# Four layers on one core: layer 0's output products moved into layer 1, transposes of layers 2 and 3 sent through DRAM

## The chip, the core and the metric

The kernel runs on one core of a Trainium2 chip. The metric is device time in microseconds of one execution, the median of several. The engines are PE (matrix products), DVE (vector), ACT (activations), POOL (general vector work) and SP, which here issues almost every DMA. Each works through its own list of instructions in order and waits on semaphores that others raise.

## What is computed

Four transformer-like layers on 8 blocks of 512 tokens with 128 features, all in float32; each layer is attention and then a feed-forward part, each on a layer-normed copy of x and added back to x.

```python
x = x + _L0_attn_ref(_layernorm(x), ...)  # spiking attention with batch norm
x = x + _L0_ffn_ref(_layernorm(x), ...)   # 8 heads x 16 small experts, the best two weighted; out @ Wo + bo
x = x + _L1_attn_ref(_layernorm(x), ...)  # linear attention
x = x + _L1_ffn_ref(_layernorm(x), ...)   # gated part and one of 8 experts on 256 chosen tokens
x = x + _L2_attn_ref(_layernorm(x), ...)  # softmax attention, 16 heads of 64
x = x + _L2_ffn_ref(_layernorm(x), ...)   # top 2 of 8 low-rank experts on the first 1024 tokens
x = x + _L3_attn_ref(_layernorm(x), ...)  # a causal convolution of 21 taps
x = x + _L3_ffn_ref(_layernorm(x), ...)   # gated part whose inputs and weights are rounded to FP4
```

In `_L3_ffn_ref` every group of 16 numbers is scaled by its largest and rounded to one of 15 values, for x (128 wide), for the weights (352 x 128) and for the hidden h (352 wide).

## The kernel before

x stays in SBUF as eight tiles x[b] of 128 partitions x 4 x 128: token row p, tile j, feature. A product needs features on the partitions, so every normed block is transposed first: four 128x128 transposes on PE by the identity (into one bank) and an ACT copy of 128x512 out of the bank.

**Layer 0's feed-forward part** is a loop over 128 units (b, e), 16 experts for each of 8 blocks (lines 689 to 706). A unit's `first_half` multiplies h by w1 (four 32-row products, four banks) and lets ACT apply Gelu in two instructions (L569 on one bank, L570 on three); `second_half`, two units later, multiplies by w2, DVE scales by the gates (L582), and POOL adds to acc[b] (L588). `finish(b)` multiplies acc[b] by Wo and adds the result to x[b] (L274); it runs in unit (b+1, 4), in a bank lent from the three that the next unit's `first_half` needs, and for the last block after the loop. There the very last product of unit 127 is not added to acc by POOL, but multiplied by Wo on its own. The gates of `choice` (steps of DVE work, one a unit, five in each of the first two) come back from DRAM, spread over partitions, by 8 DMAs for every 4 units (L550).

**Layer 1** runs rounds i over a list of stages (lines 1217 to 1238): each stage works on block i + lag, so a block's attention takes several rounds. `stats` (lag 2) is the first to read x[b].

**Layers 2 and 3** (`late`) are 64 frames n = 8 b + c (block b, pair c of heads). Per frame, in the order in which PE sees it (lines 2601 to 2619): `scores(n, 0)`, hook "V", `context(n-1)`, hook "G", `scores(n, 1)`, hook "D", `project(n)`, hook "E". Hooks hold work of other parts, put there by hand with `at(frame, hook, function)`:

- `norm_steps`: statistics, scaling on ACT, transposes (`turn_`, L1472, ACT copy L1473). `new_xt(b)` makes layer 2's input of block b this way; `project(8b-2)` is the first to need it.
- `planned(b, start)`: layer 3 of block b; start is 13, 20, 27, 34, 41, 48, 56, so three blocks are always at different stages. In frames counted from start: norm at 0 and 1, convolution taps at 2 to 4, `conv_out` and new statistics at 5, rounding of x (`quant_x1`, `quant_x2`) at z-2 and z-1, its transposes (`turn_x`, L2089) at z-1, gate products at z to z+3, rounding of h in two halves at z+1 to z+4, h turned, `down` and the store at z+6. z is 10 for the "wide" blocks 0 to 4.
- `weights_in_frames`: the weights of layer 3 are rounded in frames 1, 2 and 4 and transposed a frame later (`turned_w`, L2435 and L2445).

For the wide blocks h already goes another way: `blocks_h` lets DVE transpose within 32x32 blocks (L2154) and SP write the blocks to their places in DRAM by four DMAs in pieces of 128 bytes (L2158); `fetch_h`, a frame later in the same hook, reads the turned h back.

`project(n)` and `gate_steps` use halves of PE's rows. Their second half on the same bank must not overtake the first, and SP is the messenger:

```python
def mark(ins):
    m = nc.sync.nop(nofuse=True).ins
    tc.add_manual_dep(m, ins.name, SYNC)
    return m
```

The nop waits on SP for the last product of a first half; PE's next half waits for the nop. `gate_steps` are called inside `scores(n, 0)` (hook "S"), after about half of it.

Of the kernel before, what the change touches and what calls it, by code (L numbers as in the profile page):

```python
# [25 lines left out]
P = 128  # L26
D = 128
# [137 lines left out]
def body(ctx, tc, dram, spans, x_in, ib, it, ic, ei, out):  # L165
# [113 lines left out]

    def layer0():  # L280
# [7 lines left out]
        with ExitStack() as st:  # L288
# [7 lines left out]
            acc = once.tile([P, NB, TB], F32, tag="acc", name="acc")  # L296
# [46 lines left out]
            def scale(b, own=3):  # L343
                l0[b]["xn"] = xn = norm.tile([P, J, D], F32, tag="xn", name="xn")
                nb, rs = l0[b]["by"]
                scaled(xn, x[b], (nb, rs), own)
                for j in range(own, J):
                    r1, n1 = rs[:, j : j + 1], nb[:, j : j + 1]
                    nc.gpsimd.tensor_scalar(xn[:, j, :], x[b][:, j, :], r1, n1, ALU.mult, ALU.add)
# [89 lines left out]
            def exponentials(b):  # L439
                nc.scalar.activation(acc[:, b, :], depth[:, b, :], AF.Exp)  # L440

            def choice(b):


                d, ex = by_expert(depth, b), by_expert(acc, b)
# [43 lines left out]
            with (  # L489
# [8 lines left out]
                def run(stages, iterations):  # L498
                    for i in iterations:
# [20 lines left out]
                        (lambda b: scale(b, J), -1),  # L520
# [52 lines left out]
            def second_half(b, e, hm, gs):  # L573
                po = bank()
                for i in range(4):
                    mm(
                        po[32 * i : 32 * (i + 1), :],
                        w2[:, e, :, :].rearrange("p a o -> p (a o)"),
                        hm[:, i, :],
                    )  # L580
                pr = acc[:, b, :] if e == 0 else wp.tile([P, TB], F32, tag="pr", name="pr")
                nc.vector.scalar_tensor_tensor(  # L582
                    pr, po, f0["b2"][:, e : e + 1], gs, ALU.add, ALU.mult
                )
                if (b, e) == (NB - 1, 15):
                    l0[b]["last"] = pr
                elif e > 0:
                    nc.gpsimd.tensor_tensor(acc[:, b, :], acc[:, b, :], pr, ALU.add)  # L588

            def finish(b):  # L590
                terms = [(lambda j: acc[:, b, j * P : (j + 1) * P], f0["wo"])]
                if "last" in l0[b]:
                    terms.append((lambda j: cols(l0[b]["last"], j), f0["wo"]))
                add_to_residual(b, by_token(terms, None))
# [48 lines left out]
            with tc.manual_schedule():  # L643
# [36 lines left out]
                def second(n):  # L680

                    if n >= 2:
                        b, e = units[n - 2]
                        second_half(b, e, hms.pop(n - 2), gs[(n - 2) // 4][:, e % 4, :])
                        fetch(n - 1)
                    for _ in range(1 if n > 1 else 5):
                        side("V", n)

                for n in range(len(units) + 2):
                    first(n)  # L690
                    if n >= len(units):

                        banks["own"] = threes[0][:, 1 + n - len(units), :]
                        second(n)
                        banks.pop("own")
                        continue

                    banks["own"] = threes[(n + 1) % 2][:, 0, :]
                    b, e = units[min(n, len(units) - 1)]
                    if e == 4 and b > 0:  # L700
                        finish(b - 1)
                    else:
                        side("P", n)
                    banks.pop("own")
                    second(n)
                finish(NB - 1)
# [124 lines left out]
    def layer1():  # L831
# [9 lines left out]
        with tc.tile_pool(name="l1", bufs=2) as wp, tc.tile_pool(name="l1c", bufs=1) as once:  # L841
# [372 lines left out]
            def chosen_put():  # L1214
# [13 lines left out]
                (project_kv, 0),  # L1228
                (z_turn, -7),
# [9 lines left out]
            with tc.manual_schedule():  # L1239
# [13 lines left out]
                nought = once.tile([P, J, D], F32, tag="nought", name="nought")  # L1253
# [152 lines left out]
    def late():  # L1406
# [11 lines left out]
        with tc.tile_pool(name="a2", bufs=2) as wp, tc.tile_pool(name="l3", bufs=1) as lp:  # L1418
# [3 lines left out]
            steps = {}  # L1422

# [6 lines left out]


            def norm_steps(b, dst, bias=None, part=(0, J)):
# [41 lines left out]

                return stats, scale, turn_, t
# [512 lines left out]
            def layer3(b, xp, tile_, part=(0, J), conv_bank="one", h_tag="h"):  # L1988
# [96 lines left out]

                def turn_x():
                    ps = bank()
                    for j in range(j1 - j0):
                        nc.tensor.transpose(cols(ps, j), cols(t["xq"], j), ident)  # L2089
                    t["xt"] = xt = tile_("xt", block("xt3", 2))[:, lo:hi]  # L2090
                    nc.scalar.copy(xt, ps[:, :n])
# [53 lines left out]
                def quant_h2_tile(i, j):  # L2145
                    sc, a = t["fh", i]
                    k = slice(22 * j, 22 * (j + 1))
                    h = tile_("h", h_tile)
                    fp4_round(lp, h[:, 2 * i + j, :], sc[:, k], a[:, k, :], 22)
# [76 lines left out]
                stats, scale, turn_, _ = norm_steps(  # L2226
                    b, lambda: xp()[:, pad + lo : pad + hi], "b3", part
                )
                stats2, scale2, _, t2 = norm_steps(b, None, None, part)
                return SimpleNamespace(t=t, **{k: v for k, v in locals().items() if callable(v)})  # L2230

            def planned(b, f0_):
# [7 lines left out]
                plan = [  # L2240
                    (1, "V", s.stats) if b == 1 else (0, "E", s.stats),
                    (1, "G", s.scale),
                    (1, "E", s.turn_),
# [12 lines left out]
                else:  # L2256
# [15 lines left out]
                    (6, "E", s.quant_x1) if early else (z - 2, "V", s.quant_x1),  # L2272
                    (z - 1, "V", s.quant_x2),
                    (z - 1, "E", s.turn_x),
                ]
                for j in range(J):
# [10 lines left out]
                    (h_ + 4, "V", lambda: s.quant_h2(1)),  # L2287
                ]
                if wide:
                    plan += [  # L2290
                        (z + 2, "E", lambda: s.blocks_h(0)),
                        (z + 3, "E", lambda: s.fetch_h(0)),
                        (z + 4, "E", lambda: s.blocks_h(1)),
                        (z + 5, "E", lambda: s.fetch_h(1)),
                        (z + 6, "E", s.down),
# [12 lines left out]
            for b in range(1, NB):  # L2308
                stats, scale, turn_, _ = norm_steps(b, new_xt(b), "lb")
                n = {1: 3, 2: 6, 3: 14, 4: 26, 5: 33, 6: 40, 7: 47}[b]  # L2310
                at(n, "V" if b < 4 else "E", stats)
                at(n + 1, "G", scale)
                at(n + 1, "E", turn_)
# [24 lines left out]
            def end():  # L2338
# [63 lines left out]
                B.quant_h2_tile(1, 0)  # L2402
                B.quant_h2_tile(1, 1)
# [5 lines left out]
            def weights_in_frames():  # L2409
# [20 lines left out]
                def turned_w(name):  # L2430
                    ps = bank()
                    w_ = wq[name]
                    if name == "down":
                        for i, at_ in thirds:
                            nc.tensor.transpose(  # L2435
                                ps[:C3, i * P : (i + 1) * P], w_[:, at_ : at_ + C3], ident
                            )
                        wt["down"] = const.tile([P, 3, P], F32, tag="wd", name="wd")
                        nc.vector.tensor_copy(
                            wt["down"][:C3], ps[:C3, : 3 * P].rearrange("p (i n) -> p i n", i=3)  # L2440
                        )
                        nc.vector.memset(wt["down"][: C3 - thirds[1][1], 1:, :], 0.0)
                    else:
                        for i, w in chunks:
                            nc.tensor.transpose(  # L2445
                                ps[:, i * P : i * P + w], cols(w_, i)[:w], ident[:w, :w]
                            )
                        wt[name] = const.tile([P, I3], F32, tag="wt_" + name, name="wt_" + name)
                        nc.vector.tensor_copy(wt[name], ps[:, :I3])
# [101 lines left out]
                for frame, name in ((1, "gate"), (2, "up"), (4, "down")):  # L2551
                    at(frame, "V", lambda name=name: rounded(name))
                    at(frame + 1, "E", lambda name=name: turned_w(name))
# [30 lines left out]
            with tc.manual_schedule():  # L2584
# [16 lines left out]
                for n in range(N):  # L2601
# [17 lines left out]
                    weigh(n, 1)  # L2619
                    hook(n, "E")  # L2620
# [57 lines left out]
```

## Time and profile before

| | us |
|---|---|
| three timed runs | 1400.63, 1401.19, 1397.15 |
| median | 1400.63 |
| the profiled execution | 1393.95 |
| its span, first to last instruction | 1392.2 |
| busy: PE, DVE, ACT, POOL | 1327.5, 1014.3, 1014.6, 642.4 |
| layer 0's unit loop | about 104 to 382 |
| layer 1 | about 386 to 500 |
| frames of layers 2 and 3 | about 504 to 1334 |

A matmul's record includes its latency (a 128-column transpose lasts 0.27 us, but four of them start 0.11 us apart), so the stages are judged by the distance of starts, not by busy time. In the timelines a line's first number is its start in us from the span's start, then its duration, engine, line, operation, output<-input, shapes and count; in brackets stands how long the engine had been idle before it and whose event ended that. In rows by line, the numbers after the bar are total busy us and mean ns, then the idle time before and its causes.

### The profile page before, as it was taken

To read this page: it belongs to the slowest core of one execution; us is meant where nothing else is said; L and a number is where in the kernel's file an instruction comes from. 1 tells how busy PE (TensorE), PEld (TensorE's weight loads), DVE (VectorE), ACT (ScalarE), POOL (GpSimd) and SP (SyncE) were. 2 spreads that over 40 slices of the span, in tenths; PEclk is the share of its full clock that TensorE was granted. 3 is DMA by queue.
4 is the path that set the end of the run, shared out by engine and by line. 5 is a ranking of instruction groups with operands and counts; after the bars stand their busy time and mean duration, and the time that the engine had idled before them with its cause. 6 is when DMAs were issued, how large, how long until landed. Compare 5 with 4: busy or idle time off the path is not lost.

```text
span 1392.2 us, 33106 instructions
## 1 busy us (share of the span) xinstructions
PE 1327.5 (95%) x12935; PEld 706.1 (51%) x12935; DVE 1014.3 (73%) x2148; ACT 1014.6 (73%) x2060; POOL 642.4 (46%) x748
## 2 busy tenths in 40 slices
PE   7889999999989999999999999999999999999997
PEld 3762222222267655547447545555555545555576
DVE  6785556666467778863783778888788797887876
ACT  7869999999978656665684686787767867667632
POOL 6645666666632533330472353353443634424432
PEclk9999999999999999999999999999999999999999
DMA  5019999999681010031211101101011010010000
GB/s 180 1 27 139 141 126 127 132 127 133 85 272 32 28 40 24 16 108 33 60 31 38 45 2 22 30 2 33 20 22 24 9 33 20 19 27 9 2 8 16
DMA packets 100713, 78.14 MB, mean 56 GB/s; under 512 B 52717, under 2 KB 93581, under 8 KB 96206
## 3 DMA queue, kind: packets, MB, share of 16 engines
q1 hardware_dynamic: 98828, 72.10, 28.3%
q0 software_dynamic: 1152, 2.36, 0.6%
q8 instruction: 102, 1.67, 0.6%
q10 hardware_dynamic: 578, 1.57, 0.3%
q14 instruction: 53, 0.43, 0.1%
HBM read 59.03 MB, written 16.97 MB: 55 GB/s over the span
## 4 chain that ended last, share of the span: by engine, by line
PE 52%; ACT 22%; DVE 19%; issue 3%; POOL 2%; DMA 1%; SPq 1%; DVEq 0%; ACTq 0%; POOLq 0%
PE ps L250 41%; PE ps L1556 8%; ACT hm L570 6%; ACT ex L1635 5%; DVE nm L1629 5%; ACT hm L569 3%; ACT prod L2023 2%; PE ps L2206 1%; DVE fa L1395 1%; DVE acc L2009 1%; DVE s L732 1%; ACT h L389 1%; DVE fa L1379 1%; DVE fsc L1374 1%; ACT q L1517 1%
## 5 line engine op out<-in xcount | busy, mean ns | idle before, releaser
L1635 ACT ACTIVATE ex<-ps,nm 128x512 f32<-128x512 f32 x512 | 345.2, 687 | 172.6 <-DVE nm L1629 170.2
L1629 DVE TENSOR_REDUCE nm<-ps 128x2 f32<-128x1024 f32 x256 | 301.1, 1211 | 41.9 <-PE ps L250 41.5
L250 PE MATMUL ps<-q,k 64*64 64x512 f32 (+1 forms) x2240 | 258.3, 565 | 7.4 <-ACT ex L1635 5.4
L250 PE MATMUL ps<-ex,vs 128*64 128x512 f32 x1024 | 233.9, 599 | 1.1 <-DVE sm L1649 1.1
L1650 POOL TENSOR_TENSOR vs<-v,sm 128x256 f32<-128x256 f32 x128 | 78.6, 614 | 296.6 <-DVE sm L1649 269.6
L588 POOL TENSOR_TENSOR acc<-acc,pr 128x512 f32<-128x512 f32 x119 | 165.6, 1391 | 93.8 <-DVE pr L582 85.8
L1556 PE MATMUL ps<-xt,blob_a 64*64 64x512 f32 x912 | 207.8, 589 | 0.5 <-SPq L1523 0.5
L570 ACT ACTIVATE hm<-ps,blob_f 128x1536 f32<-128x1536 f32 x128 | 196.2, 1533 | 0.0
L582 DVE SCALAR_TENSOR_TENSOR pr<-ps,blob_f,gs 128x512 f32<-128x512 f32 x120 | 90.1, 750 | 93.7 <-PE ps L250 72.1
L250 PEld LDWEIGHTS ps<-q,k 64*64 64x64 f32 x2240 | 74.6, 132 | 150.5 <-ACT ex L1635 77.6
L250 PE MATMUL ps<-h,w 32*128 32x512 f32 x1024 | 148.3, 643 | 1.1 <-ACT hm L569 0.6
L250 PEld LDWEIGHTS ps<-ex,vs 128*64 128x64 f32 x1024 | 68.1, 137 | 152.9 <-issue 126.7
L250 PE MATMUL ps<-hm,w 128*32 128x512 f32 x1024 | 136.9, 607 | 2.3 <-DVE pr L582 2.2
L2024 POOL TENSOR_TENSOR acs<-acs,prod 128x512 f32<-128x512 f32 x96 | 124.0, 1292 | 23.9 <-ACT prod L2023 19.4
L1556 PE MATMUL ps<-blob_a,ct 64*64 64x128 f32 x1824 | 118.6, 269 | 0.0
L1556 PE MATMUL ps<-blob_a,xt 64*64 64x128 f32 x1824 | 118.6, 269 | 0.0
L1556 PEld LDWEIGHTS ps<-blob_a,ct 64*64 64x64 f32 x1824 | 106.3, 133 | 0.0
L1635 ACT ACTIVATION_READ_ACCUMULATOR ex<-ps,nm 128x1 f32 x512 | 104.9, 205 | 0.0
L1556 PEld LDWEIGHTS ps<-blob_a,xt 64*64 64x64 f32 x1824 | 103.0, 133 | 0.0
L569 ACT ACTIVATE hm<-ps,blob_f 128x512 f32<-128x512 f32 x128 | 88.0, 687 | 13.3 <-PE ps L250 13.2
L250 PEld LDWEIGHTS ps<-h,w 32*128 32x128 f32 x1024 | 41.0, 184 | 109.1 <-ACT hm L569 100.5
L1556 PEld LDWEIGHTS ps<-xt,blob_a 64*64 64x64 f32 x912 | 61.7, 133 | 32.2 <-issue 28.7
(373 smaller groups left out, 2204.5 us busy)
## 6 DMA issues: line engine op xcount, KB each, us to landing
gs<-gates SPq DMA_DIRECT2D x248, 128.0 KB, 7.4
ht<-turned_h SPq DMA_DIRECT2D x20, 180.0 KB, 3.0
turned_h<-hb SPq DMA_DIRECT2D x40, 88.0 KB, 2.3
blob_f<-in_f SPq DMA_DIRECT2D x1, 2560.0 KB, 9.0
blob_a<-in_a SPq DMA_DIRECT2D x1, 2056.0 KB, 13.5
x<-in_x SPq DMA_DIRECT2D x8, 256.0 KB, 5.8
gates<-turned SPq DMA_DIRECT2D x32, 64.0 KB, 4.7
slots_in<-nought SPq DMA_DIRECT2D x8, 256.0 KB, 4.8
```

Source lines behind the costliest of these rows:

```text
L250: nc.tensor.matmul(out_, lhs, rhs, start=start, stop=stop)
L389: nc.scalar.activation(hk, hk, AF.Sigmoid, bias=bi[:, k : k + 1], scale=sc[:, k : k + 1])
L569: nc.scalar.activation(hm[:, 0, :], p1, AF.Gelu, bias=bias)
L570: nc.scalar.activation(hm[:, 1:, :], p3, AF.Gelu, bias=bias)
L582: nc.vector.scalar_tensor_tensor(pr, po, f0["b2"][:, e : e + 1], gs, ALU.add, ALU.mult)
L588: nc.gpsimd.tensor_tensor(acc[:, b, :], acc[:, b, :], pr, ALU.add)
L1556: ins = nc.tensor.matmul(*args, **kw).ins
L1629: nc.vector.tensor_reduce(nm, ps, AX.X, ALU.max, negate=True)
L1635: nc.scalar.activation(ex[kt][:, i, :], ps[:, i, :], AF.Exp, bias=nm[:, i : i + 1], accum_out=sm[:, kt, i : i + 1],)
L1650: nc.gpsimd.tensor_tensor(vs[:, tiles, :, :], vs_[n][:, tiles, :].rearrange("p j (i n) -> p j i n", i=2), sm[:, tiles, :].unsqueeze(3).to_ ...
L2023: nc.scalar.activation(p, src, AF.Copy, scale=w)
L2024: nc.gpsimd.tensor_tensor(t["acs"], t["acs"], p, ALU.add)
```

## The change

1. `finish(0)` and `finish(1)` stay in the unit loop; `finish(2)` runs after unit 127's first half; `finish(3)` to `finish(7)` become a stage of layer 1 with lag 3, after `project_kv`. acc[3] to acc[7] move to a pool that outlives layer 0. POOL adds the last product too. In layer 0 POOL scales the fourth tile of each block in the second pass as well, and the first two units take 4 and 2 steps of `choice` instead of 5 and 5.
2. Eighteen runs of transposes in the frames become a DVE transpose in blocks, four DMAs to DRAM and a read later: layer 2's inputs of blocks 1 to 7, the norms of layer 3 of blocks 2 to 4, x rounded of blocks 0 to 4, and the three weights.
3. A new hook "F", in front of "E", holds the reads, so a frame's reads stand before its writes in SP's list.
4. The second half of h's rounding is done in two quarters, in frames z+4 and z+6 (block 4: z+5); its write and read, and `down`, move two frames (block 4: one) later. Some statistics are made earlier.

```diff
+    def finish(b):
+        wo = f0["wo"]
+        add_to_residual(b, by_token([(lambda j: cols(acc[b], j), wo)], None))
...
-            acc = once.tile([P, NB, TB], F32, tag="acc", name="acc")
+            acc.extend(once.tile([P, TB], F32, tag=f"acc{b}", name="acc") for b in range(3))
+            acc.extend(last_acc[:, b, :] for b in range(NB - 3))
...
-                        (lambda b: scale(b, J), -1),
+                        (scale, -1),
...
-                    for _ in range(1 if n > 1 else 5):
+                    for _ in range((4, 2)[n] if n < 2 else 1):
...
                     if n >= len(units):
-
-                        banks["own"] = threes[0][:, 1 + n - len(units), :]
+                        if n > len(units):
+                            banks["own"] = bank("first")
                         second(n)
+                        if n == len(units):
+                            banks["own"] = threes[0][:, 0, :]
+                            finish(2)
...
-                    if e == 4 and b > 0:
+                    if e == 4 and 0 < b < 3:
                         finish(b - 1)
...
-                finish(NB - 1)
...
                 (project_kv, 0),
+                (lambda b: b > 2 and finish(b), 3),
                 (z_turn, -7),
...
+            def in_blocks(src):
+                nc.vector.transpose(src, src)
+                far = tc.dram_tile([P, TB], F32, name=f"turned{len(fars)}")
+                fars.append(far)
+                to = far.rearrange("(c r) (j a s) -> a r j c s", c=4, j=J, a=4)
+                for a in range(4):
+                    nc.sync.dma_start(
+                        to[a],
+                        src[32 * a : 32 * (a + 1), :].rearrange("r (j c s) -> r j c s", j=J, c=4),
+                    )
+                return far
...
+                def blocks():
+                    t["far"] = in_blocks(t["xn"].rearrange("p j d -> p (j d)"))
+
+                def fetch():
+                    nc.sync.dma_start(dst(), t["far"])
...
+                def blocks_x():
+                    t["far"] = in_blocks(t["xq"])
+
+                def fetch_x():
+                    t["xt"] = xt = tile_("xt", block("xt3", 2))
+                    nc.sync.dma_start(xt, t["far"])
...
+                more = 2 if b < NB - 4 else 1
+                if 2 <= b <= 4:
+                    plan = [
+                        (-1, "E", s.stats),
+                        (0, "G", s.scale),
+                        (0, "E", s.blocks1),
+                        (1, "F", s.fetch1),
+                    ]
...
+                if wide:
+                    plan += [
+                        (z - 3, "V", s.quant_x1),
+                        (z - 2, "V", s.quant_x2),
+                        (z - 2, "E", s.blocks_x),
+                        (z - 1, "F", s.fetch_x),
+                    ]
...
-                    (h_ + 4, "V", lambda: s.quant_h2(1)),
+                    (h_ + 4, "V", lambda: s.quant_h2_tile(1, 2) if wide else s.quant_h2(1)),
+                ]
+                if wide:
+                    plan.append((h_ + 4 + more, "V", lambda: s.quant_h2_tile(1, 3)))
+                plan += [
                 ]
                 if wide:
                     plan += [
                         (z + 2, "E", lambda: s.blocks_h(0)),
-                        (z + 3, "E", lambda: s.fetch_h(0)),
-                        (z + 4, "E", lambda: s.blocks_h(1)),
-                        (z + 5, "E", lambda: s.fetch_h(1)),
-                        (z + 6, "E", s.down),
+                        (z + 3, "F", lambda: s.fetch_h(0)),
+                        (z + 4 + more, "E", lambda: s.blocks_h(1)),
+                        (z + 5 + more, "F", lambda: s.fetch_h(1)),
+                        (z + 6 + more, "E", s.down),
                     ]
...
-                n = {1: 3, 2: 6, 3: 14, 4: 26, 5: 33, 6: 40, 7: 47}[b]
+                n = {1: 3, 2: 5, 3: 14, 4: 23, 5: 30, 6: 37, 7: 44}[b]
                 at(n, "V" if b < 4 else "E", stats)
                 at(n + 1, "G", scale)
-                at(n + 1, "E", turn_)
+                blocks, fetch = t_["in turn"]
+                at(n + 1, "E", blocks)
+                at(n + 2, "F", fetch)
...
-                    at(frame + 1, "E", lambda name=name: turned_w(name))
+                    at(frame + 1, "E", lambda name=name: raw.update({(name, 0): turned_w(name)}))
+                    at(frame + 3, "F", lambda name=name: fetch_w(name, raw[name, 0]))
...
                     weigh(n, 1)
+                    hook(n, "F")
                     hook(n, "E")
```

## The prediction

> **What bounds the kernel now.** I read the busy line and the slices first, then the chain of waits, then timelines of one stretch of each stage.
>
> ```profile
> PE 1327.5 (95%) x12935; PEld 706.1 (51%) x12935; DVE 1014.3 (73%) x2148; ACT 1014.6 (73%) x2060; POOL 642.4 (46%) x748
> PE 52%; ACT 22%; DVE 19%; issue 3%; POOL 2%; DMA 1%; SPq 1%; DVEq 0%; ACTq 0%; POOLq 0%
> ```
>
> A 95% busy PE is an average over different stages. In layer 0's unit loop (105 to 380 us) the starts of L570 lie 2.067 us apart: ACT's two Gelu instructions fill the unit. Only where `finish` runs is a unit longer, 3.48 or 3.49 us, seven times (units 21, 37, ..., 117). One of them:
>
> ```profile
> 354.94 1.13 PE L250 MATMUL ps<-blob_f,acc 128*128 128x128 f32 x8 [0.29 <-ACT hm L570]
> 356.17 0.69 DVE L274 TENSOR_TENSOR x<-x,ps 128x512 f32<-128x512 f32 x1 [1.45 <-PE ps L250]
> 356.99 1.14 PE L250 MATMUL ps<-h,w 32*128 32x512 f32 x8
> 358.23 0.69 ACT L569 ACTIVATE hm<-ps,blob_f 128x512 f32<-128x512 f32 x1 [1.37 <-PE ps L250]
> ```
>
> The output product borrows the bank of the next unit, so that unit's matmuls (356.99) wait for DVE to empty it, and ACT then waits 1.37 us.
>
> In layers 2 and 3 I cut the time where `context` begins (first matmul ps<-ex,vs of each frame). A frame with nothing added takes 10.64 us (572.90 to 583.54), one with gate products 11.83 (905.57 to 917.40, 917.40 to 929.23): PE without a gap. Frames with a run of transposes take more than the run: the four transposes are 0.44 us of PE (0.11 apart), but the frames from 866.50 and 878.05 take 11.55 and 11.70, 0.91 and 1.06 over. The rest is a wait for a bank that DVE empties late. DVE limits some frames itself: the one from 929.23, with roundings, statistics and block turn, takes 14.36 for 13.6 of PE.
>
> ```profile
> L1472 PE MATMUL ps<-blob_c,xn 128*128 128x128 f32 x60 | 10.0, 282 | 3.3 <-DVE k L1518 1.3 <-ACT xn L1454 0.9
> L474 DVE STREAM_TRANSPOSE turned<-left 128x512 f32<-128x512 f32 x8 | 5.6, 702 | 0.0
> ```
>
> The first row gives latency (282 ns), not pace; the second is what replaces four such transposes and an ACT copy of about 0.6 us.
>
> SP matters most for what follows. In the products made in halves, SP's nop (`mark`, L1523) passes PE's first half on to its second, and SP works in order. Two stretches show what that costs, without and with writes in front of the nop:
>
> ```profile
> 927.28 0.17 DVE L1649 RECIPROCAL sm<-sm 128x4 f32<-128x4 f32 x1
> 927.51 0.46 PE L2206 MATMUL ps<-wt_gate,xt 64*64 64x352 f32 x2
> 928.53 0.46 PE L2206 MATMUL ps<-wt_up,xt 64*64 64x352 f32 x2
> ...
> 939.69 0.88 DVE L2154 STREAM_TRANSPOSE hb<-h 128x704 f32<-128x704 f32 x1
> 940.59 2.03 SPq L2158 DMA_DIRECT2D turned_h<-hb  x4
> 941.86 0.46 PE L2206 MATMUL ps<-wt_gate,xt 64*64 64x352 f32 x2
> 942.89 0.46 PE L2206 MATMUL ps<-wt_up,xt 64*64 64x352 f32 x2
> ```
>
> SP is busy with four writes until 942.62; its nop follows at 942.70 and PE's second half at 942.89. That was just in time, because `conv_out` (938.54, about 2 us) lay in between.
>
> **Layers 0 and 1.** (a) Five of seven `finish` calls leave the unit loop: 5 x (3.49 - 2.07) = -7.1. Bounds: 0, if gates arriving by DMA bound the loop, and -7.1. Between the last issue of a group of gates and its first use lie 9.3 to 13.8 us in these blocks, landing takes 9.5 at most; I take -7.1. (b) The first units: DVE steps of `choice` (10 before, 6 after) push the first L582 to 108.92, and ACT idles 1.54 at 110.81. I take -1.3; bounds 0 and -1.5. (c) `scale` leaves its fourth tile to POOL: 0.41 us of ACT against 0.45 of POOL (L349). The chain there is mostly DVE: -0.5; bounds -1 and +0.5. (d) The end: PE idles 0.72 waiting for POOL's sum (384.35), then runs `finish(7)` until 386.13. Both go, -2.5; `finish(2)` fits into PE's gap of 1.06 at 381.5. Bounds 0 and -2.5. (e) Layer 1 gains five products of 0.88 us PE, each with a 0.69 us DVE addition ahead of `k_map`. A round of 7.45 us (411.2 to 418.7) has 0.65 of PE gaps; the first two rounds have no `output` and more room. About +0.7 in three rounds: +2.0; bounds 0 and +3.5. Sum: -9.4.
>
> **Layers 2 and 3, the runs.** Per run PE loses 0.44 us (weights: 0.33), DVE gains 0.70, SP gains four writes at 0.57 each (L477: 64 KB in 128-byte pieces, like these) and one read of about 0.4 (L2566). Reads issue a frame after the writes, which land in 2.3 us, so they wait for nothing; about 3 us later they are there, and only x for the gates (used some 3 us after) is close. What I expect of frames, without the SP nop:
>
> - three weights and xt of blocks 1 and 2: 0.68, 0.7, 0.70, 0.88, 0.92 over today; -3.7 of 3.9, as DVE has room there;
> - xt of block 3: -0.8; x of block 0: -0.95, but +0.6 in the frame before, which DVE fills (789.91, 14.63 us);
> - three turns of seven frames (866.50 to 954.45 and the next two), each: 11.55 to 10.8, 11.70 to 10.64, and 15.83, less the 2.64 of `down` that moves, from 13.19 to 11.85: -3.15; together -9.45;
> - the end of this part: xt of block 7 -0.9, x of block 4 -1.34, the split rounding -0.8.
>
> Together -17.9. `down` in its new frame, four times +0.3 for DVE's late banks: +1.2. With +0.6 above: -16.1. Pure PE time alone would be 15 x 0.44 + 3 x 0.33 = -7.6, the other end.
>
> The ACT copies that go cost nothing today (ACT has idle time in every frame); the later `fetch` and `down` frames delay only output. The half roundings add some 0.3 us of DVE per block and take 1.4 from a full frame.
>
> **The SP queue.** `blocks_h(1)` moves two frames later (frames 29, 36, 43, 50; 56 for block 4), and the next frame there begins with a gate product in halves; before, none did. xt of block 4 (frame 24) is written ahead of one too. From the reference stretch: sm ends at 927.45, the block turn would end at 928.3, SP's four writes at 930.4, the second half at 930.6 instead of 928.53: +2.05 us, six times, +12.3. Nothing covers these six; `down` covers frames 31, 38, 45, `conv_out` 25, 32, 39, 46. The trace has no uncovered case, so bounds: 0 (PE late anyway) and 3.5 (one such write took 1.82 instead of 0.54, at 1117). I take 2.05, from the nearest rows.
>
> [...] The trace's pace of 0.11 us is what I count with. [...]
>
> **Sum.** -9.4 - 16.1 + 12.3 = -13.2. Against the profiled execution's 1393.95 us (span 1392.2 and 1.75 around it): 1380.7. The three timed runs have a median of 1400.63, 6.7 more; taken off that: 1387.4, so **1387**.
>
> **Rivals.** *The nop costs nothing*: PE is late in these six frames for other reasons, or the writes issue sooner. For it: the trace's waits for SP add up to only 2.4 us. Against: every write ahead of a nop was covered there. -25.5, 1375. *DVE becomes the bound*: the 15 turns of 0.70 us all end on the path, +10.5: -2.7, 1398. For it: frames with much DVE work already run over. Against: in most frames that get a turn DVE was idle for over 1 us. *Layer 0 does not get faster*, because the loop is then held by its gates (DMA share 0.97 to 0.99 there): -6.1, 1394.5; against it, the slack above. *Slower: the relay holds PE in other frames too*. The other 12 writes also stand ahead of the nops of `project`, some 7 us into the next frame; if DVE reaches its turns that late, each costs another 2.05. From seven such on the gain is gone; all twelve give +11.4, 1412. For it: one queue, 72 more writes of 0.57 us. Against: in the reference frames DVE reaches the end-of-frame work within 1 us of PE.
>
> **Chances.** Forecast (1382 to 1392) 0.40; no cost of the nop (1372 to 1382) 0.25; layer 0 not faster 0.12; DVE 0.13; slower 0.10. The range 1373 to 1399 leaves out the slower case and the tails of two others. About 0.3% (4.2 us) is what a measurement of this kernel can tell from no change. Faster by more (below 1396.4): the first three and a sliver of DVE's, 0.78; within: 0.12; slower: 0.10.
>
> **What would show it.** Unit starts of 2.07 at units 53 to 117; layer 1 rounds of about 8 us; frames of 10.7 where 11.6 stood; the second gate half about 2 us late, after four writes, in six places; no L2445, L2435, and few L2089 and L1472. Wrong, if frames of 10.64 us grow (DVE), or PE waits for SP inside `project`.

## The result, and the profile after

| us | before | after |
|---|---|---|
| median of nine runs | 1399.49 (1396.57 to 1401.19) | 1403.06 (1400.57 to 1405.35) |
| the profiled execution | 1393.95 | 1400.57 |
| layer 0's unit loop, first to last large Gelu (L570, after: L578) | 103.72 to 380.33 | 102.67 to 378.95 |
| start of the first frame (its first `context`) | 515.78 | 518.35 |
| frames, first to last | 814.14 | 817.82 |

The changed kernel takes 1.0027 times as long (95% interval 1.0016 to 1.0037): 3 to 4 us slower, where the forecast was 13 us faster. By the traces neither half has gained: +2.6 us up to the first frame, +3.7 in the frames (the profiled executions differ by 6.6, the medians by 3.6; the last section says where some of such spread comes from).

The page of the changed kernel, its busy line and its chain:

```profile
PE 1320.6 (94%) x12858; PEld 698.4 (50%) x12858; DVE 1022.4 (73%) x2182; ACT 1007.1 (72%) x2037; POOL 649.9 (46%) x763
PE 39%; DVE 14%; ACT 7%; issue 2%; SPq 1%; POOL 1%; DMA 0%; DVEq 0%; ACTq 0%; POOLq 0%
```

PE has 6.9 us less to do, yet the span is 6.6 us longer: the time is in PE's waits. Two rows show that the transposes moved: 20 instead of 60 on PE for the norms, and 10 of normed x on DVE in one of the new places. Two more show the unit where `finish(2)` stood: its large Gelu starts 2.07 us after the one before, where it was 3.49 (this distance is what I call the length of a unit).

```profile
L1437 DVE STREAM_TRANSPOSE xn<-xn 128x512 f32<-128x512 f32 x10 | 6.9, 691 | 0.0
...
L1488 PE MATMUL ps<-blob_c,xn 128*128 128x128 f32 x20 | 3.7, 287 | 2.8 <-DVE k L1541 1.6 <-ACT xn L1470 0.9
```

```profile
220.34 1.53 ACT L578 ACTIVATE hm<-ps,blob_f 128x1536 f32<-128x1536 f32 x1
...
222.41 1.53 ACT L578 ACTIVATE hm<-ps,blob_f 128x1536 f32<-128x1536 f32 x1
```

**New wait one: SP in front of the gate products.** PE's waits for SP (us in total, times, longest; PEld is PE's loading of weights, and the two rows see largely the same stalls, so they do not add up); in the kernel before, all waits for SP came to 2.4 us:

```profile
PEld ps L2236 <- SPq L1546: 14.1, 9, 3.3
PE ps L2236 <- SPq L1546: 10.0, 7, 2.8
```

One of them, in frame 35 (I number frames by the `context` that begins them, so frame 35 holds hook E of n = 36 and the first scores, with hook S, of n = 37):

```profile
992.27 0.88 DVE L2184 STREAM_TRANSPOSE hb<-h 128x704 f32<-128x704 f32 x1
992.76 0.51 PE L2236 MATMUL ps<-wt_gate,xt 64*64 64x352 f32 x2
...
993.18 2.05 SPq L2188 DMA_DIRECT2D turned_h<-hb  x4
...
995.34 0.51 PE L2236 MATMUL ps<-wt_up,xt 64*64 64x352 f32 x2 [1.32 <-SPq L1546]
```

The first halves run at 992.76; SP is busy issuing four writes until 995.23, and only then its nop lets the second halves go. It is the stall that the prediction priced.

**New wait two: the gates of block 1.** The timeline of unit 20 and what precedes it on SP:

```profile
125.97 4.48 SPq L485 DMA_DIRECT2D gates<-turned  x4
134.24 17.41 SPq L558 DMA_DIRECT2D gs<-gates  x22
...
145.74 0.75 DVE L590 SCALAR_TENSOR_TENSOR acc<-ps,blob_f,gs 128x512 f32<-128x512 f32 x1 [4.59 <-DMA gs<-gates]
...
146.54 1.93 PE L250 MATMUL ps<-hm,w 128*32 128x512 f32 x8 [4.13 <-DVE acc L590]
148.41 2.09 PE L250 MATMUL ps<-h,w 32*128 32x512 f32 x8
...
150.59 0.69 ACT L577 ACTIVATE hm<-ps,blob_f 128x512 f32<-128x512 f32 x1 [5.97 <-PE ps L250]
```

The write of block 1's gates (L485) is issued at 125.97, behind all reads of group 3; the first reads of block 1 (L558) need it landed and follow at 134.24 (before: 128.53). DVE then waits 4.59 us for them, and unit 20 takes 8.09 us instead of 2.07.

### The profile page after: what moved, and what is told of

Same layout as the page of the kernel before. It is cut to its first block, busy times and chain, and to the rows that moved or that the text cites. A ratio compares the mean times of both kernels' runs of the same rounds, so it can differ in the third digit from the quotient of the medians.

```text
span 1398.8 us, 33151 instructions
## 1 busy us (share of the span) xinstructions
PE 1320.6 (94%) x12858; PEld 698.4 (50%) x12858; DVE 1022.4 (73%) x2182; ACT 1007.1 (72%) x2037; POOL 649.9 (46%) x763
## 4 chain that ended last, share of the span: by engine, by line
PE 39%; DVE 14%; ACT 7%; issue 2%; SPq 1%; POOL 1%; DMA 0%; DVEq 0%; ACTq 0%; POOLq 0%
PE ps L250 28%; PE ps L1579 9%; ACT ex L1658 5%; DVE nm L1652 5%; PE ps L2236 1%; DVE v L1526 1%; SPq L2188 1%; DVE acc L2032 1%; DVE fa L1382 1%; DVE fsc L1377 1%; DVE s L1458 1%; ACT xn L1470 1%; DVE fa L1398 1%; DVE k L1541 1%; DVE fa L1399 0%
## 5 line engine op out<-in xcount | busy, mean ns | idle before, releaser
L578 ACT ACTIVATE hm<-ps,blob_f 128x1536 f32<-128x1536 f32 x128 | 196.3, 1534 | 0.0
L2047 POOL TENSOR_TENSOR acs<-acs,prod 128x512 f32<-128x512 f32 x96 | 123.4, 1286 | 12.7 <-ACT prod L2046 7.6
L577 ACT ACTIVATE hm<-ps,blob_f 128x512 f32<-128x512 f32 x128 | 88.1, 688 | 13.2 <-PE ps L250 13.0
```

The lines of the kernel that those rows point to most:

```text
L577: nc.scalar.activation(hm[:, 0, :], p1, AF.Gelu, bias=bias)
L578: nc.scalar.activation(hm[:, 1:, :], p3, AF.Gelu, bias=bias)
L2047: nc.gpsimd.tensor_tensor(t["acs"], t["acs"], p, ALU.add)
```

## Experiments

**Theory** from these traces: (1) SP's writes in front of the relay cost some 12 us; (2) fewer steps of `choice` at the start delay the write of block 1's gates and cost 5 to 7; (3) the transposes bring less than counted, as DVE decides the frames that got them. **Rivals**: the loop is held by its gates' traffic as such; the frames are held by DVE or by banks, whatever SP does; the gain in the frames is the new order of the work and not the transposes.

Times of all runs, against runs of the kernel before on the same chip:

| run | median us | before | ratio (95% interval) |
|---|---|---|---|
| e1_choice | 1396.56 | 1395.41 | 1.0007 (0.9992 to 1.0022) |
| e2_writes | 1387.78 | 1395.41 | 0.9943 (0.9925 to 0.9961) |
| e3_frames | 1397.42 | 1395.41 | 1.0012 (0.9998 to 1.0025) |
| e4_both | 1384.52 | 1395.41 | 0.9918 (0.9887 to 0.9949) |
| e5_triple | 1396.85 | 1396.27 | 1.0001 (0.9989 to 1.0013) |
| e6_norm3 | 1389.17 | 1396.27 | 0.9944 (0.9922 to 0.9966) |
| e7_x | 1387.85 | 1396.27 | 0.9942 (0.9925 to 0.9960) |
| e8_half | 1395.81 | 1396.27 | 0.9989 (0.9977 to 1.0001) |
| e9_choice8 | 1382.57 | 1396.11 | 0.9892 (0.9869 to 0.9916) |
| e10_front | 1387.38 | 1396.11 | 0.9936 (0.9918 to 0.9954) |
| e11_spread | 1382.22 | 1396.11 | 0.9905 (0.9885 to 0.9924) |
| e12_split | 1408.71 | 1396.69 | 1.0092 (1.0068 to 1.0116) |
| e13_all_pe | 1400.92 | 1397.39 | 1.0038 (1.0023 to 1.0053) |
| e14_norms_before | 1390.27 | 1395.52 | 0.9968 (0.9956 to 0.9980) |

Frames of the traces (us), the ones that tell the runs apart; frame 35 stands for 42 and 49, frame 33 for 40:

| frame | before | after | e2 | e14 | e8 |
|---|---|---|---|---|---|
| 3 | 11.52 | 10.64 | 10.64 | 11.52 | 10.64 |
| 4 | 11.34 | 11.46 | 11.45 | 10.64 | 11.45 |
| 23 | 11.83 | 14.84 | 12.79 | 11.83 | 12.77 |
| 30 | 11.83 | 15.41 | 15.33 | 14.93 | 12.78 |
| 33 | 11.55 | 11.53 | 11.52 | 12.01 | 13.23 |
| 34 | 11.69 | 10.64 | 10.64 | 11.52 | 10.77 |
| 35 | 15.83 | 13.72 | 12.21 | 12.64 | 14.93 |
| all | 814.14 | 817.82 | 803.74 | 810.85 | 815.81 |

### e1: the steps of choice put back

```diff
-                    for _ in range((4, 2)[n] if n < 2 else 1):
+                    for _ in range(1 if n > 1 else 5):
```

> The changed kernel with the first two units' steps of choice put back to 5 and 5. Theory (the later end of the first choice puts the write of block 1's gates behind the reads of group 3 on SP, and unit 20 waits for them): unit 20 falls from 8.1 us to about 2.1, the first frame starts near 512 us instead of 518.35, and the time falls by 5 to 7 us, to about 1397. Rival (the loop is held by the DMA traffic of the gates as such): the wait comes up again at other units, at most 1.5 us are gained, 1401.5 to 1403.

The ratio falls from 1.0027 to 1.0007, 2.8 us, though the two intervals overlap a little; in the trace the loop falls from 276.28 to 272.09 us. Unit 20 is 2.07 us again. DVE's waits for gates (us in total, times, longest), after and e1:

```profile
DVE acc L590 <- DMA gs<-gates: 11.2, 6, 4.6
DVE pr L590 <- DMA gs<-gates: 5.0, 4, 1.9
```

```profile
DVE acc L590 <- DMA gs<-gates: 4.0, 4, 2.1
DVE pr L590 <- DMA gs<-gates: 2.6, 2, 1.3
```

The theory holds, at a smaller size than expected: with ten steps at once units 2 to 4 are late again (2.86, 3.94 and 2.45 us), which gives 3 us back.

### e2: the writes behind the relay

```diff
                         (z + 4 + more, "E", lambda: s.blocks_h(1)),
+                        (z + 5 + more, "V", lambda: s.write_h(1)),
...
-                at(n + 1, "E", blocks)
+                if b < 4:
+                    at(n + 1, "E", blocks)
+                else:
+                    at(n + 1, "E", lambda blocks=blocks: blocks(True))
+                    at(n + 2, "V", t_["write"])
```

`write_h` and `write` hold the four DMAs alone; the DVE transpose stays where it was.

> The changed kernel with the writes of the second half of h and of layer 2's inputs of blocks 4 to 7 issued after the next frame's first scores (hook V) instead of at the frame's end; the DVE transposes and the reads stay where they are. Theory (four writes on SP in front of the relay of the gate products cost about 12 us): the waits of the gate products for SP fall below 2 us in all, the frames of 14.8 to 16.1 us get 0.5 to 3 us shorter, and the time falls by 9 to 13 us, to about 1392. Rival (those frames are held by DVE or by banks that come free late): the waits for SP go but their time comes up as waits for DVE; the gain is 0 to 3 us, 1400 to 1403.

The ratio is 0.9943 against 1.0027: 11.7 us. No wait of PE for SP is left, and no other wait grows in its place. The same spot of frame 35:

```profile
986.01 0.88 DVE L2195 STREAM_TRANSPOSE hb<-h 128x704 f32<-128x704 f32 x1
...
986.55 0.51 PE L2253 MATMUL ps<-wt_gate,xt 64*64 64x352 f32 x2
...
987.50 2.06 SPq L2205 DMA_DIRECT2D turned_h<-hb  x4
987.60 0.49 PE L2253 MATMUL ps<-wt_up,xt 64*64 64x352 f32 x2
```

SP issues the same writes in the same 2.06 us, now at the moment the relay is through. Per frame, after against e2: 1.5 to 1.7 in frames 35, 42 and 49, 2.05 in frame 23, 1.1 in frame 55; in frames 30, 37 and 44, where `down` covers, 0.1 to 0.7; and 3.2 in frame 28, where the four writes took SP 3.56 us in the changed kernel's trace and PE waited 2.82 (in e3's trace, with these writes at their usual 2.0 us, frame 28 takes 13.72, 1.7 more than in e2). Frame 11 is 1.7 us longer in the changed kernel's trace than in any other; PE waits for DVE there and SP issues nothing; the cause is not known.

### e3 and e10: the halves apart

e3 takes layers 0 and 1 from the kernel before and the frames as changed; e10 the same with the frames of e2.

> Layers 0 and 1 as before, layers 2 and 3 as changed. Theory (both halves of the change cost time): the first frame starts near 515.8 us, the frames last as in the changed kernel (814.9 us from the first to the 64th context against 811.2), and the time is about 2.6 us below the changed kernel, 1400.5, still 1 to 4 us above the kernel before. Rival 1 (all the loss is in layers 0 and 1): at or below the kernel before, 1399 or less. Rival 2 (all of it in the frames): 1403 or more.

> Layers 0 and 1 as in the kernel before, layers 2 and 3 as changed with the writes behind the relay. It gives what the change of layers 0 and 1 is worth once its gates come in time. From the traces (unit loop 4.9 us shorter, layer 1 and the tail 2.0 to 2.8 longer): 2 to 3 us above the kernel with both edits. If moving finish into layer 1 is worth what the prediction counted: 8 to 9 us above. If it only moves work: equal within 1 us.

e3 is 1.0012, between the two kernels and not clearly apart from either: by this, both halves lose a little. e10 lies 2.9 us above e4 (2.5 by the ratios, whose intervals overlap; its first frame starts 2.6 us later), as expected from the traces: with the gates of block 1 in time, the new layers 0 and 1 are worth about 3 us, not 8 to 9.

### e4: both edits

> Both edits together: steps of choice 5 and 5, and the writes behind the relay. If the two costs are independent: the sum of the two gains, 14 to 20 us below the changed kernel, 1383 to 1389, and so 10 to 16 us below the kernel before. If one hides the other or the frames are held by DVE: 1394 to 1399.

1384.52, ratio 0.9918; from e2 to e4 3.3 us, about what e1 gave (2.8). The two costs are independent within this spread. Loop 272.8 us against 276.6 before; from its end to layer 1's first product 4.34 against 5.91; from its end to the first frame 137.50 against 135.44. So the loop gains 3.8, the tail 1.6, and layer 1 loses 3.6.

### e9 and e11: choice earlier, and spread

```diff
-                choices = [(choice(b), 16 * (b - 1) - 5) for b in range(1, NB)]
+                choices = [(choice(b), 16 * (b - 1) - 8) for b in range(1, NB)]
```

> On top of both edits, choice of blocks 2 to 7 starts three units earlier (16 (b - 1) - 8 instead of - 5), so that on SP the write of a block's gates stands in front of the last group of reads of the block before instead of behind it. Theory (the waits of about 1 us at units 100 and 116, new since finish left the loop, come from this write and not from the reads' traffic): both fall below 0.2 us, the loop gets about 2 us shorter, the time 2 us lower. Rival (the loop is now as fast as its gates can arrive): the waits stay or move to other units, no change within 1 us.

SP's work around the start of block 6, in e4 and then in e9:

```profile
296.56 3.26 SPq L485 DMA_DIRECT2D gates<-turned  x4
303.46 6.49 SPq L558 DMA_DIRECT2D gs<-gates  x12
```

```profile
282.89 2.60 SPq L485 DMA_DIRECT2D gates<-turned  x4
286.40 28.47 SPq L558 DMA_DIRECT2D gs<-gates  x32
```

In e4 SP waits 3.6 us for the write to land before it may read; in e9 it has another group's reads to issue meanwhile. The waits at units 100 (3.40 us) and 116 (3.33 us) are gone, DVE waits 2.9 us for gates in the whole loop (e4: 7.2), and the loop takes 270.1 us. The median is 1382.57, 1.95 below e4; against their own runs of the kernel before, 0.9892 and 0.9918, with overlapping intervals. What held these two units was the place of one write in SP's list, not the traffic.

e11 also spreads the first choice: `(3, 3, 2, 2, 2)[n] if n < 5 else 1` steps.

> As the run with the earlier choices, and the first choice's twelve steps spread as 3, 3, 2, 2, 2 over five units instead of 5, 5, 1, 1. The write of block 1's gates is still issued in front of group 3's reads. Theory (the first units are late because ten DVE steps stand in front of the first products; spread, they fit): units 2 to 4 take 2.1 us instead of 2.8, 3.9 and 2.5, a gain of 2 to 3 us over the run with the earlier choices. Rival (the sum of DVE's work in the first units decides, wherever it stands): 0 to 1 us.

Units 2, 3 and 6 take 2.87, 2.60 and 2.93; the loop is 1.4 us shorter than in e9, the time the same (1382.22). Inconclusive, nearer to the rival.

### e5, e6, e7: DVE's turns tripled, or taken back

e5 does the in-place transpose three times (`for _ in range(3)`). e6 puts `turn_` in the place of `blocks1`; e7 puts `(z - 1, "E", s.turn_x)` in the place of `blocks_x` and `fetch_x`. All on top of e4.

> On top of both edits, every block transpose of x on DVE (15 of them, not the weights and h) is done three times instead of once, in place, which leaves the same result and adds 30 times 0.70 us of DVE. Theory (DVE decides the frames that got a turn): those frames grow by 1.0 to 1.4 us each, 15 to 21 us in all, to about 1402. Rival (DVE has room in most frames): only the frames whose DVE is already busy for over 11 us grow, 3 to 8 us in all, 1388 to 1393.

> On top of both edits, the norms of layer 3 of blocks 2 to 4 are transposed by PE again, in the same frame; DVE loses 0.70 us and SP four writes and a read there. Theory (the frames of 11.53 to 11.70 us with 12.5 to 13.0 us of DVE are DVE's, so moving this transpose bought nothing): these three frames keep their length within 0.3 us or get shorter, the time stays within 1 us of the kernel with both edits. Rival (each run taken off PE is worth the 0.75 to 1.06 us that the prediction counted): three frames grow by that, 2 to 3 us more.

> On top of both edits, the rounded x of blocks 0 to 4 is transposed by PE again, a frame later (the rounding stays where it is). The prediction counted 0.95 us for block 0, 1.34 for the four others: if that is right the time grows by 5 to 7 us. If only PE's own 0.44 us counts: by 2 us. If DVE decides: by 0 or less.

e5: 12.3 us slower for 21 us of added DVE, 12.7 in the frames; between theory and rival. Frames 4, 6, 24, 27, 28, 34, 35, 41 and 42 grow by 0.9 to 1.5 each, frames 3, 23, 30 and 37 by nothing. e6: frames 26, 33 and 40 grow by 0.46 to 0.48, so my theory that this transpose buys nothing fell; but it buys no more than that, 1.4 us in the three. By the medians e6 is 4.6 us slower, more than theory or rival said; 1.4 of it stands in frame 28 of its trace, where the read of the turned x landed late and PE waited 1.49 us for it, and the rest is not explained. e7: frames 35, 42 and 49 grow by 0.4 to 0.6, all frames together by 1.5; by the medians it is 3.3. The prediction's 5 to 7 does not show in the frames.

### e8 and e12: the split rounding, without it and alone

e8, on top of e4, rounds the second half of h at once, with `more = 0`, so its write and `down` go back to their old frames too. e12 makes only part 4 of the change (the split rounding and the later `down`), on the kernel before, with the write behind the relay.

> On top of both edits, the second half of h is rounded at once in the frame where it was, and its write, its read and down stand where they stood in the kernel before, two frames (block 4: one) earlier than in the changed kernel. If splitting the rounding and moving down gains what the prediction counted (0.8 for the roundings and minus 1.2 for down), the time stays within 1 us. If down costs 3.1 to 3.5 us in its new frames against 3.3 in its old one, and the split rounding takes 0.3 to 0.9 off five frames: 1 to 4 us slower. If the moves only cost: 2 to 4 us faster.

> The kernel before with only part 4 of the change: the second half of h rounded in two quarters, its write, read and down two frames later (block 4: one), the write behind the relay; all eighteen runs of transposes stay on PE, layers 0 and 1 as before. Theory (the split gains what the run with whole roundings lost, because it frees DVE in frames that the block turns fill; without the turns there is less to free): 2 to 5 us below the kernel before, 1391 to 1394. Rival 1 (the split by itself is the gain, the turns add nothing): 8 to 10 us below. Rival 2 (what the prediction counted, 0.8 less and 1.2 more for down): within 1 us.

Neither was foreseen. Without part 4, the new kernel loses 11.3 us of its gain; with part 4 alone, the old kernel loses 12.0. One frame at a time: the windows of frame 33 in e4 and then in e8 (columns: us, then busy us of PE, PEld, DVE, ACT, POOL, then the granted clock, DMA share and GB/s):

```profile
949.78:961.31 11.53, 11.13 (x133) 5.43 (x129) 10.82 (x23) 8.46 (x23) 5.05 (x8) 1.00 0.01 2
```

```profile
954.56:967.79 13.23, 11.14 (x134) 5.43 (x130) 12.52 (x23) 8.45 (x23) 5.65 (x8) 1.00 0.01 2
```

DVE's busy time grows by 1.70 and the frame by 1.70; PE's is the same. In e8 the frame is DVE's; DVE has the same 0.71 us of idle time in both. The changed layout has brought the rounding of x a frame earlier, into frames 26 and 33, and the split makes room for it there. In e12 the rounding of x stays where it was, and the last quarter and the block turn of h come to stand beside it in frames 28, 35, 42 and 49. PE's waits in e12 and its window of frame 35:

```profile
PE ps L2089 <- DVE k L1518: 11.3, 5, 2.8
```

```profile
982.95:1000.02 17.07, 14.31 (x161) 7.66 (x157) 14.53 (x22) 12.01 (x29) 7.64 (x8) 0.90 0.02 4
```

The transposes of x on PE (L2089) wait for a bank that a late DVE empties, up to 2.8 us. Frames 35 and 42 take 17.07 us, frames 28 and 49 some 15.4. The granted clock over the window is 0.90 in frame 35 and 1.00 in the other three, so it does not tell why 35 and 42 take 1.7 us more; that stays open. `down` itself moves at no gain: from e8 to e4, 2.6 to 2.9 us less in frames 35 and 49, 2.6 to 3.1 more in 37 and 51.

### e13 and e14: all fifteen back on PE

```diff
-                at(n + 1, "E", blocks)
-                at(n + 2, "F", fetch)
+                at(n + 1, "E", turn_)
```

and e6's and e7's edits, on top of e4 (whose `V` writes of these blocks go as well); the weights stay on DVE. e14 also puts `stats`, `scale` and `turn_` of layer 3's norms and of block 2's input back to their old frames.

> The kernel with both edits, with all fifteen transposes of x on PE again (the three of weights stay on DVE), the inputs of blocks 4 to 7 in the frames of the kernel before (27, 34, 41, 48); the split rounding, the earlier rounding of x, down and layers 0 and 1 stay as in the kernel with both edits. If a run taken off PE is worth PE's own 0.44 to 0.5 us: 6 to 8 us above the kernel with both edits, 1390 to 1393. If it is worth the 0.75 to 1.34 that the prediction counted: 12 to 15 us above, 1396 to 1400. If the gain is the order of the work alone: within 2 us, 1384 to 1387.

> As the run with all fifteen transposes of x on PE, but the norms (layer 2's inputs and layer 3's norms) stand in the frames of the kernel before too, so that no frame gets two of them; split rounding, earlier rounding of x, down, weights and layers 0 and 1 as in the kernel with both edits. If a run on PE costs PE's own 0.44 to 0.5 us: 6 to 8 us above the kernel with both edits, 1390 to 1393. If 0.75 to 1.34 each, as the prediction counted: 12 to 15 us above, 1396 to 1400. If the gain is the order of the work alone: within 2 us, 1384 to 1387.

e13 tells nothing on its question: I had put two runs of transposes and two scalings into frames 26, 33 and 40, which grew to 17.2 us. e14 keeps them apart: 1390.27, 5.8 us above e4 (7.0 by the ratios), and 5.7 in the frames. That is 0.38 us for each of the fifteen runs on the mean; the next section shows that single frames are far from it. e14 takes back the frames of the norms too, so its 5.7 us are the transposes and this order together; a gain by order alone, within 2 us of e4, does not fit it. Its window of frame 33, against e4's 11.53 above:

```profile
952.03:964.04 12.01, 11.46 (x136) 5.94 (x132) 11.27 (x31) 8.92 (x24) 5.27 (x9) 1.00 0.01 1
```

## Why the prediction was wrong

**The runs of transposes: the step that failed.** The fifteen runs of x were counted at -15.0 (the -17.9 without 2.1 for the weights and 0.8 for the split), 0.75 to 1.34 us a run: the whole excess of the frame that loses the run. The DVE turn in the frame where it then stands was put at nothing, but for 0.6 in one frame ("DVE has room there"). e14 less e4 gives 5.7 us. Frames that only lose a run do get 0.88 shorter (3, 27, 34 and 41), nearly as counted, the wait for the bank included. Those that lose the turn of the rounded x get 0.4 to 0.6 shorter, not 1.34, and the frames where a DVE turn now stands get longer: frame 4 by 0.82, frames 23, 30, 37, 44 and 48 by 0.4 to 0.9. All frames together: some 9.3 us won, 3.6 given back. The start of frame 4, in e4 and then in e14:

```profile
556.42 0.68 DVE L1496 STREAM_TRANSPOSE xn<-xn 128x512 f32<-128x512 f32 x1
557.03 2.32 DVE L1663 TENSOR_REDUCE nm<-ps 128x2 f32<-128x1024 f32 x2
557.10 3.65 PE L250 MATMUL ps<-ex,vs 128*64 128x512 f32 x16
...
558.31 0.69 ACT L1669 ACTIVATE ex<-ps,nm 128x512 f32<-128x512 f32 x1 [2.12 <-DVE nm L1663]
```

```profile
558.21 2.36 DVE L1663 TENSOR_REDUCE nm<-ps 128x2 f32<-128x1024 f32 x2 [0.75 <-PE ps L250]
558.93 3.65 PE L250 MATMUL ps<-ex,vs 128*64 128x512 f32 x16
559.53 0.69 ACT L1669 ACTIVATE ex<-ps,nm 128x512 f32<-128x512 f32 x1 [1.78 <-DVE nm L1663]
```

In e4 the turn stands in front of the maxima (L1663) that the next exponentials need: ACT starts these 1.21 us after `context`, in e14 0.60. PE then waits for ACT: in the changed kernel's trace, with the same turn in frame 4, PE's next scores wait 0.25 us for the exponentials and their loading of weights 1.13 (at 572.23). With the turn done three times (e5), frames 4 and 6 get another 1.5 us longer. e13, which has the statistics that also came into frame 4 but its transposes on PE, takes 10.85 us there: 0.6 of the 0.82 are the turn's, 0.2 the statistics'. In e14 DVE is busy for 8.67 of that frame's 10.64 us, so room in the frame as a whole does not make a turn free. In frames 23, 30 and 37 tripling adds nothing; statistics came into these frames too, and what makes these frames longer stays open. "Pure PE time alone", -7.6 for all eighteen, is close to the -7.9 measured (5.7, and 2.2 for the weights), but by luck: a weight brings 0.7 and not 0.33, the inputs of blocks 1 to 3 next to nothing, others 0.9.

The other terms:

- **The split rounding (-0.8), `down` (+1.2) and the fuller frame (+0.6): small in the sum, but not a sum.** From the kernel before to e14 the frames lose 3.3 us, 2.2 of them by the weights; all the other moves together give -1.1, where +1.0 was counted, so the miss is not here. But the terms can't be added one by one: part 4 gains 11 us in e8's kernel and loses 12 in e12's, since each frame takes either the roundings of x or those of h.
- **The SP queue: right, its number in part by luck.** +12.3 forecast, 11.7 measured (e2). The six places are as named, but the stalls are 1.1 to 2.05 us and once 3.2, and `down` left up to 0.7 us uncovered in three more; with 1.7 for the 3.2, as in e3, the six come to 9.6. The slower rival, the relay inside `project`, did not occur: no wait of PE for SP stands at a line of `project`.
- **The first units (b): wrong in sign.** -1.3 forecast. The gain itself came (unit 3 takes 2.04 us instead of 3.70), but the step looked at DVE's load in the first units and not at what those steps produce. They end in a DMA, which now comes behind the next reads on SP: +2.8 us in all (e1), and 4.2 in the trace's loop. Its "bounds 0 and -1.5" left out a loss altogether.
- **Five `finish` (a): the mechanism right, the size -5.1 for -7.1** (e4's trace, from unit 20 on). The units are 2.07 us, but units 100 and 116 then take 3.40 and 3.33, as they wait for gates. The text's own figures, 9.3 us from issue to use against up to 9.5 for landing, left no room for that. The rival "held by its gates" was right about the wait and not about its cause: e9 shows that it is the order on SP, where a longer unit had covered the write.
- **The start (c): as counted or better.** -0.5 forecast; the first large Gelu starts at 101.95 to 103.38 in the traces with the new layer 0, at 103.72 to 104.42 with the old.
- **The tail and layer 1 (d, e): mis-sized.** -1.6 for -2.5, as `finish(2)` did not fit into PE's gap (in e4 the last hm product starts 3.34 us after the last large Gelu, with `finish(2)` in front of it; before: 2.24), and +3.6 for +2.0. Three rounds lengthen by 0.6 as counted, but the first round, which I took to have room, loses 0.8, and about 1 us more is lost in the later part, where the traces of the two kernels differ without a cause that I found. Layers 0 and 1 sum to -9.4 in the forecast; the runs give -2.9 for them with the gates of block 1 in time (e4 less e10), and +0.4 to +2 as they are (e2 less e10, the changed kernel less e3).

Together: forecast -9.4 - 16.1 + 12.3; measured about +1, -8.7 (e10) and +11.7, some +4, beside the +3.6 of the result. Each rival changed one of these terms and kept the others; none had layer 0 and the frames fall short at once.

With the two faults undone and `choice` earlier, the change is worth having: e9, at 1382.57, is 13.5 us faster than the kernel before and by the two ratios some 19 faster than the changed one. That this is about the 13.2 of the forecast is chance, for its terms are others.

## What to carry to other kernels

When work leaves a loop, ask which transfer had used the time it took: in a list that one engine works through in order, as SP does here, look for the write that something later reads, and put other issues between the two (SP waited 3.6 us for such a write in e4, and unit 20 took 8.09 us for 2.07 in the changed kernel). Price a transpose that moves from PE to DVE in two frames: what the one gains that loses it (0.4 to 0.9 us here), and what the one pays where the DVE turn then stands (0 to 0.9), by asking which instruction has to wait behind it; DVE's idle time in that frame is not enough to go by (frame 4 has 1.97 us of it in e14 and pays 0.82). Where two edits meet in one engine's full frame, price the frame, not the edits. A nop that relays between PE's halves belongs ahead of the writes in SP's list (1.1 to 2.05 us a time here, 3.2 where the four writes took SP 3.56).

## What the runs showed of the hardware

The long wait of PE in unit 20 cost more than itself. The windows of unit 20 in the changed kernel (columns as above):

```profile
142.00:144.00 2.00, 0.41 (x4) 0.00 (x0) 0.00 (x0) 2.00 (x3) 1.31 (x2) 1.00 1.01 131
144.00:146.00 2.00, 0.00 (x0) 0.00 (x0) 0.26 (x1) 0.63 (x1) 0.00 (x0) 0.68 1.05 135
146.00:148.00 2.00, 1.46 (x8) 0.20 (x8) 1.08 (x2) 0.00 (x0) 0.00 (x0) 0.50 1.04 135
148.00:150.00 2.00, 2.00 (x12) 0.52 (x8) 1.35 (x2) 0.00 (x0) 0.62 (x1) 0.50 1.05 135
150.00:152.00 2.00, 2.00 (x12) 1.49 (x8) 0.00 (x0) 1.41 (x2) 1.02 (x1) 0.61 1.04 135
```

PE is idle for 4.13 us, and the clock that it is granted falls to 0.50, from 2.3 us after PE stopped (about 144.7) until about 151.5; its eight products take 1.93 us where they take 1.06 elsewhere in the loop. The unit is 6.0 us longer, for a stall of 4.1. The slow stretch lasts 6.8 us, and PE works in the last five of them. The clock fell a second time, at about 390.5, after a gap of 1.93 us that began at 387.8; a gap of 2.82 us in frame 28 (from 904.5) was followed by no fall, with 1.00 in the windows from 904 to 912. So in this trace the length of a gap does not by itself tell whether the clock falls.

Such stretches also go some way to explain why these executions differ. After the gap at 387.8, between layers 0 and 1, the changed kernel's trace has a clock of 0.62 and 0.52 in the windows from 390 to 394, and a round of layer 1 takes 8.8 us; e4's trace has no such stretch there, and the same round takes 7.5. Over the nine runs of the changed kernel the mean clock goes from 0.996 (1400.57 us) to 0.993 (1405.35 us), though runs of 0.994 lie anywhere from 1401.76 to 1405.0; the profiled execution of the kernel before had 0.998, and lay 5.5 us below that kernel's median. So a difference of 2 us between two single traces was not taken as an effect here unless the same lines showed it frame by frame.
